# Queries and keys by seven half products, sums on GpSimd, divisions on ScalarE, and output groups spread over the steps

## The chip, the cores and the metric

The kernel runs on one core of a Trainium2 chip. The core has a matrix engine (TensorE, PE in the profile, with PEld for its weight loads), a vector engine (VectorE, DVE), a scalar engine (ScalarE, ACT), a general engine (GpSimd, POOL) and a queue engine that issues transfers (SyncE, SP). They run at the same time and wait for one another by semaphores. The metric is the device time of the whole program in microseconds. The three runs of the kernel before took 3513.65, 3513.8 and 3515.68 us, a median of 3513.8.

## The reference, cut to what matters

Two attention layers follow each other. Each normalises its input by groups, projects it to queries, keys and values, adds relative-position terms to the scores, and adds the projected output to its input. There are 4 images of 32 x 32 tokens with 768 channels, and 12 heads of 64 channels. All of it is float32.

```python
qkv = x @ Wqkv                                   # (4, 1024, 768) @ (768, 2304)
q, k, v = split by 3, heads of 64
rel_h = einsum('bhwc,hkc->bhwk', r_q, Rh)        # position terms from the queries
rel_w = einsum('bhwc,wkc->bhwk', r_q, Rw)
scores = scale * (q @ k.T) + rel_h[..., :, None] + rel_w[..., None, :]
out = softmax(scores) @ v
x = x + (out @ Wproj + bproj)
```

In the second layer the projections have a bias, and the scale is applied to q as well.

## The kernel before, in words

**Tiling.** An image of one layer is 6 chunks of 128 channels by 1024 tokens. The 8 image passes (2 layers of 4 images) are numbered `im`. The heads go in pairs: 6 pairs per pass, 48 in all, numbered `g`. A pair's scores are cut into 8 units of 128 query rows, numbered `n`; a unit holds both heads. So there are 384 steps, each of one unit, in the loop over `units` (L562).

**What a step holds.** The engines' order is written by hand (`manual_schedule`, L539): each engine does its instructions in the order of the Python calls. In a step for unit `n` of pair `g` come: the small things left over from two steps before (`early`), the position terms of the unit two ahead (`biases`, GpSimd, L323), the scores of the unit one ahead (`scores`: L337 on TensorE, L346 on VectorE which adds the position terms and takes the row's extreme, L350 on ScalarE for the exponential), the reads of turned probabilities that are due (`behind`), the transposition of unit `n` (`turn`: L370 on VectorE, its write to memory L372 on SP), the division of the unit one ahead (`divide`: L358, one head on GpSimd at L362 and one on ScalarE at L364), and then a share of other matrix work out of a list `todo` (`take`). In step 6 and in step 2 of the next pair `weigh` multiplies the probabilities with the values (L399, `av`). What it reads from memory, `pt`, is fetched a quarter (two units) at a time by `read_back` (L381): units 0 and 1 in step 3, 2 and 3 in step 4, 4 and 5 in step 7, 6 and 7 in step 0 of the next pair.

**The list of other matrix work.** `prepare(g + 1)` gives the projections of the next pair: `project_in` makes queries and keys, each in two halves of 512 tokens (L215); `project_values` makes the values of two pairs in four groups, two of them per pair (L250). `put_out` gives groups of the output projection (L471), four per pair, 12 steps of `take` together. `shares` (L567) says how many pieces are taken in each step: 6, 6, 0, 6, 12, 6, 0, 12. So in a usual pair the queries are made in steps 0 and 1, the keys in 3 and 4, values in 4 and 5, and all the output groups in step 7.

**Half-height matmuls.** L215 and L250 split each chunk of 128 channels into two halves of 64 rows. The two halves go to different row halves of the matrix engine and to two accumulators, and a ScalarE copy (L228 or L230) and a VectorE sum (L231) bring them together. The scores (L337) and the position products (L282, `tp`) also use half the rows, for one head each. The output projection uses all 128 rows.

**Buffers.** `ps_m` has two accumulators for all groups but the scores, so a group's accumulator is wanted again two groups later. `ps_s` has two for the scores of the two heads. The position products go through memory: `positions` copies a part of them, ScalarE writes it (L289), and `diagonals` reads it back shifted, in eight reads of SP (L309) for the whole pair, into `rel`, which `biases` reads.

**Between images.** The statistics of the next image are collected during pairs 0 to 2, its group statistics are exchanged in pair 3 (`norm`), and its chunks are normalised by VectorE in pair 4 (`apply`, L194).

Of the kernel before, what the change touches and what calls it, by code (L numbers as in the profile page):

```python
# [50 lines left out]
AHEAD = 3  # L51
# [3 lines left out]
def attention_blocks(ctx: ExitStack, tc: tile.TileContext, a: dict, out: bass.AP):  # L55
# [4 lines left out]
    wpool = ctx.enter_context(tc.tile_pool(name="weights", bufs=2))  # L60
    wopool = ctx.enter_context(tc.tile_pool(name="wo", bufs=2))
    xpool = ctx.enter_context(tc.tile_pool(name="x", bufs=NC + AHEAD))
    apool = ctx.enter_context(tc.tile_pool(name="attn", bufs=6))
    qkpool = ctx.enter_context(tc.tile_pool(name="qk", bufs=2))
    vpool = ctx.enter_context(tc.tile_pool(name="v", bufs=3))
    scpool = ctx.enter_context(tc.tile_pool(name="sc", bufs=6))
    tmppool = ctx.enter_context(tc.tile_pool(name="tmp", bufs=2))
    tbpool = ctx.enter_context(tc.tile_pool(name="tb", bufs=2))
    ptpool = ctx.enter_context(tc.tile_pool(name="pt", bufs=2))
    relpool = ctx.enter_context(tc.tile_pool(name="rel", bufs=2))  # L70
    iopool = ctx.enter_context(tc.tile_pool(name="io", bufs=4))
# [15 lines left out]
    xn_of, w_of, wo_of = {im: [] for im in range(NI)}, {}, {}  # L87

    def load_x(im, c, chunk=None):

        l, b = images[im]
        if c == len(xn_of[im]):
            xn_of[im].append(xpool.tile([P, S], FP, tag="xn", name=f"xn_{im}_{c}"))
        chunk = c if chunk is None else chunk
        nc.sync.dma_start(out=xn_of[im][c], in_=srcs[l][b][chunk * P : (chunk + 1) * P, :])

    def load_w(g, which):

        im, pair = divmod(g, NP)
        if which == 2:  # L100
            w = wpool.tile([P, NC, 2 * P], FP, tag="wv", bufs=1, name=f"wv_{g}")
            src = a[f"wv{images[im][0]}"][pair // 2]
        else:
            w = wpool.tile([P, NC, P], FP, tag="w", name=f"w_{g}_{which}")
            src = a[f"wqk{images[im][0]}"][pair, which]
        w_of[g, which] = w
        nc.sync.dma_start(out=w, in_=src.rearrange("p (c o) -> p c o", c=NC))

    for c in range(NC):
        load_x(0, c)  # L110
    for which in range(3):
        load_w(0, which)
# [35 lines left out]
    def stats(im, c, i, x):  # L148

        if i == 0:  # L150
            half_stats[im] = small.tile([P, 2, 6], FP, tag="st", name=f"st_{im}_{c}")
        st = half_stats[im]
        nc.vector.bn_stats(st[:, i, :], x)  # L153
        if i == 1:
            nc.vector.bn_aggr(mv_of[im][:, c, :], st.rearrange("p i s -> p (i s)"))

    def norm(im):
# [26 lines left out]
        def inverses():  # L184
            nc.vector.reciprocal(mv[:, 2, 0:1], mv[:, 2, 1:2])
            for k, x in enumerate((mv[:, 0, 0:1], mv[:, 2, 0:1])):
                nc.vector.tensor_copy(g[:, 1, :, k], x.to_broadcast([NG, GS]))
# [5 lines left out]
        def apply(c):  # L193
            nc.vector.tensor_scalar(  # L194
                xn_of[im][c], xn_of[im][c], nrm[:, c, 0:1], nrm[:, c, 1:2], ALU.subtract, ALU.mult
            )

        return {1: gather, 2: by_group, 4: groups, 5: inverses, 7: spread}, apply

# [3 lines left out]
    def project_in(g, which, i):  # L203

        im, pair = divmod(g, NP)
        xn, w = xn_of[im], w_of[g, which]
        cols = slice(i * HALF, (i + 1) * HALF)
        if i == 0:
            tag = "qk"[which]
            qk_of[g, which] = qkpool.tile([P, S], FP, tag=tag, name=f"{tag}_{g}")  # L210
        t = ps_m.tile([P, 2, HALF], FP, tag="m", name=f"pj_{g}_{which}_{i}")
        for c in range(NC):
            for a in range(2):
                rows = slice(a * D, (a + 1) * D)
                nc.tensor.matmul(  # L215
                    t[:, a, :], lhsT=w[rows, c, :], rhs=xn[c][rows, cols],
                    start=(c == 0), stop=(c == NC - 1),
                )
            if c < NC - 1:
                yield True  # L220
# [49 lines left out]
    def positions(g, i):  # L270
# [27 lines left out]
        if i == 1:  # L298
            later.append(lambda: diagonals(g))
# [386 lines left out]
```

## Time and profile before

| | |
|---|---|
| median of three runs | 3513.8 us |
| the profiled execution, its own time | 3513.09 us |
| span from the first to the last instruction | 3511.3 us |
| granted TensorE clock | 0.998 |
| PE busy | 3460.9 us, 99% of the span |
| DVE busy | 2306.5 us, 66% |
| POOL busy | 2290.3 us, 65% |
| ACT busy | 1810.3 us, 52% |
| transfers, share of 16 engines (largest queue) | 82.9% |

A line of the groups view gives the line of the code, the engine, the operation, what it writes and reads, the shape and the count; then the busy time and the mean of one in ns; then the idle time just before, with what ended it. A line of the chain of work that ended last gives shares of the span. A line of a timeline gives the start, the length and what ran. Each matmul of the code is two instructions in the profile. Matmul ends are modelled, so distances between starts say more than busy time.

### The profile page before, as it was taken

How to read it: one execution, taken by the hardware profiler on the slowest of the kernel's cores; microseconds unless marked ns; L12 is line 12 of the kernel's file. 1: busy time of each engine (PE TensorE's matmuls, PEld its weight loads, DVE VectorE, ACT ScalarE, POOL GpSimd, SP SyncE). 2: the span in 40 equal slices, each digit the busy share in tenths (PEclk: the TensorE clock that was granted, in tenths of full speed). 3: DMA queues.
4: the chain of work that ended last, by engine and by line, in shares of the span. 5: the costliest groups of instructions: out<-in, count | busy, mean ns of one | idle time of the engine just before them, and what ended most of it. 6: DMA issues, size and time to landing. Idle time of an engine off the chain costs nothing.

```text
span 3511.3 us, 55069 instructions
## 1 busy us (share of the span) xinstructions
PE 3460.9 (99%) x21120; PEld 1920.0 (55%) x21120; DVE 2306.5 (66%) x3532; ACT 1810.3 (52%) x2913; POOL 2290.3 (65%) x1154
## 2 busy tenths in 40 slices
PE   6999999999999999999999999999999999999998
PEld 3555555555555555555555555555555555555553
DVE  4766767767677676666766667666666666666665
ACT  3555545554545545455545555455545555455543
POOL 3776666666666666666666666666666666666662
PEclk9999999999999999999999999999999999999999
DMA  3988988889898888988888988888888888888877
GB/s 129 321 299 290 322 306 308 316 285 316 301 321 308 295 313 290 320 303 285 310 306 314 305 287 309 311 305 300 297 305 316 307 292 301 310 297 291 293 275 264
DMA packets 520407, 1046.75 MB, mean 298 GB/s; under 512 B 142672, under 2 KB 205648, under 8 KB 470992
## 3 DMA queue, kind: packets, MB, share of 16 engines
q1 hardware_dynamic: 465648, 1015.81, 82.9%
q10 hardware_dynamic: 54496, 27.43, 2.6%
q8 instruction: 166, 2.72, 0.3%
q14 instruction: 97, 0.79, 0.1%
HBM read 568.01 MB, written 475.10 MB: 297 GB/s over the span
## 4 chain that ended last, share of the span: by engine, by line
PE 94%; DVE 2%; DMA 2%; issue 1%; ACT 0%; SPq 0%; DVEq 0%; ACTq 0%
PE pj L215 26%; PE av L399 19%; PE s L337 19%; PE pv L250 14%; PE o L471 14%; PE tp L282 2%; DMA td<-tb 1%; DVE tb L370 1%; DVE sc L346 1%; DMA pt<-td 0%; DVE st L153 0%; DVE q L231 0%; DVE res L482 0%; DMA per<-mv 0%; ACT q L230 0%
## 5 line engine op out<-in xcount | busy, mean ns | idle before, releaser
L323 POOL TENSOR_TENSOR sc<-rel 128x1024 f32<-128x1024 f32 x768 | 1881.2, 2473 | 48.3 <-DMA rel<-tdr 33.6
L350 ACT ACTIVATE sc<-sc,sm 128x1024 f32<-128x1024 f32 x768 | 880.3, 1147 | 792.1 <-DVE sm L346 790.6
L346 DVE CUSTOM_DVE_ANT_0 sc<-s,sc 128x1024 f32<-128x1024 f32 x768 | 908.2, 1220 | 438.3 <-issue 221.5
L362 POOL TENSOR_SCALAR sc<-sc,sm 128x1024 f32<-128x1024 f32 x376 | 420.3, 1118 | 1099.5 <-DVE sm L358 1069.0
L215 PE MATMUL pj<-xn,w 64*128 64x512 f32 x4608 | 1032.5, 591 | 26.9 <-DVE xn L194 25.9
L370 DVE STREAM_TRANSPOSE tb<-sc 128x1024 f32<-128x1024 f32 x768 | 907.9, 1220 | 14.6 <-DMA td<-tb 12.9
L215 PEld LDWEIGHTS pj<-xn,w 64*128 64x128 f32 x4608 | 452.2, 188 | 569.3 <-issue 527.6
L337 PE MATMUL s<-k,q 64*128 64x512 f32 x3072 | 751.1, 598 | 6.6 <-DVE sm L346 6.4
L364 ACT ACTIVATE sc<-sc,sm 128x1024 f32<-128x1024 f32 x392 | 449.2, 1148 | 499.6 <-DVE sm L358 499.6
L399 PE MATMUL av<-pt,v 128*64 128x256 f32 x6144 | 684.7, 381 | 10.1 <-DVE q L231 7.7
L399 PEld LDWEIGHTS av<-pt,v 128*64 128x64 f32 x6144 | 432.9, 137 | 291.6 <-DVE q L231 41.6
L250 PE MATMUL pv<-wv,xn 64*128 64x256 f32 x4608 | 515.7, 376 | 0.0
L250 PEld LDWEIGHTS pv<-wv,xn 64*128 64x128 f32 x4608 | 448.7, 187 | 90.5 <-issue 33.4
L471 PE MATMUL o<-attn,wo 128*128 128x512 f32 x1080 | 476.3, 597 | 0.0
L337 PEld LDWEIGHTS s<-k,q 64*128 64x128 f32 x3072 | 288.7, 187 | 299.9 <-issue 268.8
L471 PEld LDWEIGHTS o<-attn,wo 128*128 128x128 f32 x1080 | 201.5, 190 | 271.4 <-issue 254.9
L261 DVE TENSOR_TENSOR v<-pv,v 128x256 f32<-128x256 f32 x192 | 81.5, 425 | 240.1 <-ACT v L260 240.1
L231 DVE TENSOR_TENSOR k<-pj,k 128x512 f32<-128x512 f32 x96 | 66.4, 692 | 182.3 <-ACT k L228 93.1
L231 DVE TENSOR_TENSOR q<-pj,q 128x512 f32<-128x512 f32 x96 | 66.4, 692 | 171.8 <-ACT q L230 85.9
L260 ACT COPY v<-pv 128x256 f32<-128x256 f32 x192 | 70.5, 367 | 189.8 <-PE pv L250 142.7
L297 ACT COPY rel<-tp 32x256 f32<-32x256 f32 x384 | 139.4, 363 | 53.9 <-ACT t L287 27.8
L350 ACT ACTIVATION_READ_ACCUMULATOR sc<-sc,sm 128x1 f32 x768 | 143.2, 187 | 0.0
(36 smaller groups left out, 941.7 us busy)
## 6 DMA issues: line engine op xcount, KB each, us to landing
td<-tb SPq DMA_DIRECT2D x384, 1024.0 KB, 5.7
pt<-td SPq DMA_DIRECT2D x382, 1024.0 KB, 8.8
w<-in_wqk SPq DMA_DIRECT2D x96, 384.0 KB, 5.7
tdr<-t ACTq DMA_DIRECT2D x96, 256.0 KB, 8.0
part<-res SPq DMA_DIRECT2D x84, 256.0 KB, 4.7
res<-part SPq DMA_DIRECT2D x84, 256.0 KB, 7.5
wv<-in_wv SPq DMA_DIRECT2D x24, 768.0 KB, 6.6
wo<-in_wo SPq DMA_DIRECT2D x90, 192.0 KB, 7.1
```

What stands on the lines that cost most here:

```text
L215: nc.tensor.matmul(t[:, a, :], lhsT=w[rows, c, :], rhs=xn[c][rows, cols], start=(c == 0), stop=(c == NC - 1),)
L250: nc.tensor.matmul(t[:, a, k, :], lhsT=xn[c][rows, (2 * i + k) * P : (2 * i + k + 1) * P], rhs=w[rows, c, :], start=(c == 0), stop=(c == N ...
L297: nc.scalar.copy(rel_of[g][rows, :, 0, 4 * i : 4 * i + 4, :], src)
L323: nc.gpsimd.tensor_tensor(sc.rearrange("p (a k) (u l) -> p a (k u) l", a=4, l=8), rel[:, h, 0, n, :].unsqueeze(1).unsqueeze(3).to_broadcas ...
L337: nc.tensor.matmul(ps[h][:, cols], lhsT=q[rows, n * P : (n + 1) * P], rhs=k[rows, cols], start=True, stop=True,)
L346: nc.vector.tensor_tensor_reduce(out=sc, in0=ps[h], in1=sc, scale=-scale, scalar=BIG, op0=ALU.add, op1=ALU.min, accum_out=st[:, 0, h : h + 1],
L350: nc.scalar.activation(sc, sc, AF.Exp, bias=st[:, 0, h : h + 1], scale=-1.0, accum_out=st[:, 1, h : h + 1],)
L362: nc.gpsimd.tensor_scalar(sc, sc, st[:, 2, h : h + 1], 1.0, ALU.mult, ALU.mult)
L364: nc.scalar.mul(sc, sc, st[:, 2, h : h + 1])
L370: nc.vector.transpose(tb[:, :, h, :], sc_of[g, n, h])
L399: nc.tensor.matmul(av[rows, at * 2 * P : (at + 1) * 2 * P], lhsT=v_of[g][:, k, rows], rhs=pt_of[g, quarter].rearrange("p n r k h i -> p (n ...
L471: nc.tensor.matmul(t, lhsT=wo_of[im, o, c], rhs=attn_of[im * NP + c][:, cols], start=(c == c0), stop=(c == c1 - 1),)
```

## The change: what it does

Queries and keys together are one product of the normalised image with a weight matrix of 256 columns. It is now cut in two along all three sides: the tokens in halves x0 and x1, the channels in chunks 0 to 2 and 3 to 5, and the columns in queries (`wa`) and keys (`wc`). That would be eight products of half matrices. The changed kernel computes them as seven, from sums and differences of the halves (the scheme of Strassen and Winograd). Each of the seven is three matmuls over whole chunks of 128 rows.

GpSimd makes the sums of operands: of the weights once per pair (`combine`), of the image once per image (`sums`, spread over the steps in `sum_steps`), and of the value weights once per two pairs (`combine_values`), since the second half of the image is kept as a sum afterwards. VectorE adds up the products (seven sums per pair in place of four, L293 and L295 of the changed kernel), and ScalarE keeps one copy of a product in place of four. The bias of the second layer is added in VectorE's sums.

The divisions of both heads go to ScalarE, except for the first head of units 2 and 4, which stays on GpSimd. Normalisation goes to ScalarE (`scale` and `bias` of an activation) in pair 4, and is spread over the steps in `applies`. The image is held and loaded in halves of tokens. The diagonals are read in two halves of eight reads each, the first in step 3 and the second in step 0 of the pair itself. The list of other matrix work is mixed by `merge`: product 0 and one output group, values, values, product 1, one output group, products 2 and 3, two output groups, with shares 9, 6, 0, 6, 9, 9, 0, 6. In the opening, all groups of pair 0 are done ahead of the loop.

```diff
-    wpool = ctx.enter_context(tc.tile_pool(name="weights", bufs=2))
+    wpool = ctx.enter_context(tc.tile_pool(name="weights", bufs=1))
-    xpool = ctx.enter_context(tc.tile_pool(name="x", bufs=NC + AHEAD))
+    xpool = ctx.enter_context(tc.tile_pool(name="x", bufs=3 * NC))
-    vpool = ctx.enter_context(tc.tile_pool(name="v", bufs=3))
+    vpool = ctx.enter_context(tc.tile_pool(name="v", bufs=4))
-    tmppool = ctx.enter_context(tc.tile_pool(name="tmp", bufs=2))
+    tmppool = ctx.enter_context(tc.tile_pool(name="tmp", bufs=1))
+    spool = ctx.enter_context(tc.tile_pool(name="sums", bufs=NC // 2))
...
+    def combine(g, stage):
+
+        wa, wc, t1, t2, t4 = (weights_of(g, name) for name in "ac124")
+        sub = lambda to, x, y: nc.gpsimd.tensor_tensor(to, x, y, ALU.subtract)
+        if stage == 0:
+            sub(t1, wc[:, :NB], wa[:, :NB])
+            sub(wc[:, :NB], wc[:, NB:], wc[:, :NB])
+        else:
+            sub(t2, wc[:, NB:], t1)
+            sub(t4, wa[:, NB:], t2)
+
+    def combine_values(g):
+
+        w = wv_of[g]
+        nc.gpsimd.tensor_tensor(w[:, NB:], w[:, NB:], w[:, :NB], ALU.subtract)
...
-        def apply(c):
-            nc.vector.tensor_scalar(
-                xn_of[im][c], xn_of[im][c], nrm[:, c, 0:1], nrm[:, c, 1:2], ALU.subtract, ALU.mult
+        def apply(c, h, scalar=True):
+            x = xn_of[im][h][c]
+            if scalar:
+                nc.scalar.activation(x, x, AF.Identity, bias=nrm[:, c, 1:2], scale=nrm[:, c, 0:1])
+            else:
+                nc.vector.tensor_scalar(
+                    x, x, nrm[:, c, 0:1], nrm[:, c, 1:2], ALU.mult, ALU.add
+                )
...
+    def sums(im, which, c):
...
+        to, x, y = {
+            1: lambda: (x1[c], x1[c], x1[c + NB]),
+            2: lambda: (s(2), x1[c], x0[c]),
+            3: lambda: (s(3), x0[c], x1[c]),
+            4: lambda: (s(4), x0[c + NB], s(2)),
+        }[which]()
+        nc.gpsimd.tensor_tensor(to, x, y, ALU.add if which == 1 else ALU.subtract)
...
-    def project_in(g, which, i):
+    def products(g, kind):
...
+        ops = {
+            0: ((wa, x0), (wa[:, NB:], x0[NB:])),
+            1: ((t2, s2), (wc, s3)),
+            2: ((t1, x1), (t4, x1[NB:])),
+            3: ((wc[:, NB:], s4),),
+        }[kind]
+        for h, (w, x) in enumerate(ops):
+            for c in range(NB):
                 nc.tensor.matmul(
-                    t[:, a, :], lhsT=w[rows, c, :], rhs=xn[c][rows, cols],
-                    start=(c == 0), stop=(c == NC - 1),
+                    t[:, h, :], lhsT=w[:, c, :], rhs=x[c], start=(c == 0), stop=(c == NB - 1),
                 )
...
+        ts = [turned(x) for x in ts]
+        if kind == 0:
+            nc.scalar.copy(kept, ts[0])
+            add(turned(qs[0]), ts[1], kept, 0)
+            (later if g else mid).append(lambda: positions(g, 0))
+        elif kind == 1:
+            add(ks[0], ts[0], kept)
+            add(ks[1], ts[1], ks[0])
+        elif kind == 2:
+            add(turned(qs[1]), ts[1], ks[1], 0)
+            add(ks[0], ts[0], ks[0])
+            add(ks[1], ts[0], ks[1], 1)
+            (later if g else mid).append(lambda: positions(g, 1))
+        else:
+            add(ks[0], ts[0], ks[0], 1)
...
-        if i == 1:
-            later.append(lambda: diagonals(g))
+        later.append(lambda: diagonals(g, i))
...
-            if h == 0 and not last:
+            if h == 0 and n in (2, 4) and not last:
                 nc.gpsimd.tensor_scalar(sc, sc, st[:, 2, h : h + 1], 1.0, ALU.mult, ALU.mult)
             else:
                 nc.scalar.mul(sc, sc, st[:, 2, h : h + 1])
...
+        values = [(project_values(first, i + k), NC) for k in range(2)]
+        groups = [(products(g, kind), NC if kind < 3 else NB) for kind in range(4)]
+        return groups[:1] + values + groups[1:]
+
+    def merge(ins, outs):
+
+        if not ins or not outs:
+            return ins + outs
+        return ins[:1] + outs[:1] + ins[1:4] + outs[1:2] + ins[4:] + outs[2:]
...
+    applies = {
+        2: ((0, 0), (0, 1), (0, 2)), 3: ((0, 3),), 4: ((0, 4), (0, 5), (1, 0)),
+        5: ((1, 3), (1, 1), (1, 4)), 7: ((1, 2), (1, 5)),
+    }
+    sum_steps = {
+        (4, 5): ((3, 0),),
+        (4, 6): ((1, 0), (2, 0), (3, 1)),
+        (4, 7): ((1, 1), (2, 1)),
+        (5, 0): ((3, 2), (1, 2), (2, 2)),
+        (5, 1): ((4, 0),),
+        (5, 2): ((4, 1), (4, 2)),
+    }
...
-                shares = [6, 6, 0, 6, 12, 6, 0, 12]
+                shares = [9, 6, 0, 6, 9, 9, 0, 6] if g >= 3 else [6, 6, 0, 6, 6, 9, 0, 0]
...
+            if n in (0, 2) and g + 1 < NPAIR:
+                combine(g + 1, n // 2)
+            if n == 4 and pair % 2 and g + 1 < NPAIR:
+                combine_values(g + 1)
+            if pair == 4 and not end:
+                for h, c in applies.get(n, ()):
+                    apply(c, h)
+            if not end:
+                for which, c in sum_steps.get((pair, n), ()):
+                    sums(im + 1, which, c)
             take(todo, share)
```

## The prediction

> **What bounds the kernel now.** I read the page first: part 1 for the busy shares, part 4 for what carries the end.
>
> ```profile
> PE 3460.9 (99%) x21120; PEld 1920.0 (55%) x21120; DVE 2306.5 (66%) x3532; ACT 1810.3 (52%) x2913; POOL 2290.3 (65%) x1154
> ...
> PE 94%; DVE 2%; DMA 2%; issue 1%; ACT 0%; SPq 0%; DVEq 0%; ACTq 0%
> PE pj L215 26%; PE av L399 19%; PE s L337 19%; PE pv L250 14%; PE o L471 14%; PE tp L282 2%; DMA td<-tb 1%; DVE tb L370 1%; DVE sc L346 1%; DMA pt<-td 0%; DVE st L153 0%; DVE q L231 0%; DVE res L482 0%; DMA per<-mv 0%; ACT q L230 0%
> ```
>
> TensorE is the bound, everything else has a third of its time free, and the lines edited (`pj`) are 26% of the chain. Busy matmul ends are modelled, so I priced from starts: the timeline of TensorE, over one pair of heads in the middle (start, us, group).
>
> ```profile
> 1528.76 1.88 PE L337 MATMUL s<-k,q 64*128 64x512 f32 x8
> 1530.58 7.13 PE L399 MATMUL av<-pt,v 128*64 128x256 f32 x64
> 1537.63 1.99 PE L337 MATMUL s<-k,q 64*128 64x512 f32 x8
> 1539.55 10.57 PE L471 MATMUL o<-attn,wo 128*128 128x512 f32 x24
> 1550.05 1.99 PE L337 MATMUL s<-k,q 64*128 64x512 f32 x8
> 1551.87 5.32 PE L215 MATMUL pj<-xn,w 64*128 64x512 f32 x24
> 1557.02 1.88 PE L337 MATMUL s<-k,q 64*128 64x512 f32 x8
> 1558.74 5.32 PE L215 MATMUL pj<-xn,w 64*128 64x512 f32 x24
> 1563.89 1.06 PE L282 MATMUL tp<-tab,q 64*128 64x128 f32 x16
> 1564.78 1.89 PE L337 MATMUL s<-k,q 64*128 64x512 f32 x8
> 1566.59 7.13 PE L399 MATMUL av<-pt,v 128*64 128x256 f32 x64
> 1573.65 1.16 PE L282 MATMUL tp<-tab,q 64*128 64x128 f32 x16
> ```
>
> Groups follow without a hole. A pair takes 71.7 us (scores at 1502.95 and again at 1574.65). A matmul in the code is two instructions here (4608 `pj` for 48 x 48). The `pj` group of 24 half-height instructions takes 5.15 us, 0.429 per two; the 24 full-height ones of `o` take 10.50.
>
> The groups view prices the other engines.
>
> ```profile
> L323 POOL TENSOR_TENSOR sc<-rel 128x1024 f32<-128x1024 f32 x768 | 1881.2, 2473 | 48.3 <-DMA rel<-tdr 33.6 <-DVE tb L370 14.7
> L362 POOL TENSOR_SCALAR sc<-sc,sm 128x1024 f32<-128x1024 f32 x376 | 420.3, 1118 | 1099.5 <-DVE sm L358 1069.0 <-DMA td<-tb 30.5
> L364 ACT ACTIVATE sc<-sc,sm 128x1024 f32<-128x1024 f32 x392 | 449.2, 1148 | 499.6 <-DVE sm L358 499.6
> L194 DVE TENSOR_SCALAR xn<-xn,nrm 128x1024 f32<-128x1024 f32 x48 | 84.0, 1770 | 3.5 <-DMA nrm<-back 3.5
> L231 DVE TENSOR_TENSOR q<-pj,q 128x512 f32<-128x512 f32 x96 | 66.4, 692 | 171.8 <-ACT q L230 85.9 <-ACT q L228 85.8
> ```
>
> Last, the timelines of VectorE and of SP for two dates that the new order leans on: the last eviction of a value group, and the eight reads of the position diagonals.
>
> ```profile
> 1530.92 0.42 DVE L261 TENSOR_TENSOR v<-pv,v 128x256 f32<-128x256 f32 x1 [0.44 <-ACT v L260]
> ```
> ```profile
> 1513.15 4.13 SPq L309 DMA_DIRECT2D rel<-tdr  x8
> ```
>
> **What the skill says.** The Trainium skill, TensorEngine Tiling (Array Packing), Key Properties: row tiles run in parallel, but changing the tiling mode drains the engine. The trace agrees and prices it: weight loads inside the `o` block stand 0.429 us apart, so 24 cost 10.30; two score blocks among row-tiled work cost 1.72 each (1557.02 to 1558.74); but scores, `o`, scores take 14.24 (1537.63 to 1551.87). The excess is 0.50, and 0.11 of it is the way out of `av` (`tp` takes 1.00 after `av`, 0.89 otherwise). **A full-height block costs 0.39 us to enter and leave.** SBUF — State Buffer, Who interferes with whom: a VectorE tensor_scalar in a two-port mode and a GpSimd operation lock each other out; L194 takes 806 ns at least and 1770 in the mean, which agrees.
>
> **The change, part by part.** S is the start of a step's scores.
>
> *1. Seven products.* Per pair 48 matmuls over half chunks become 21 over whole ones. 4608 x 0.2146 = 989 us become 2016 x 0.429 = 865: -123.5. Half-height work ran two at a time, so nothing is lost by it before; all the gain is the eighth product (20.6 to 18.0 us per pair).
>
> *2. Mode switches.* Full-height blocks per pair: now one (`o`). After, in the emitted order: product 0 with an output group (step 0), product 1 with an output group (4), products 2 and 3 (5), two output groups (7): four. Over the run, 44 pairs with outputs gain three, three early ones gain three, the opening two: 143 x 0.39 = +56.
>
> *3. Image boundaries.* The DVE normalisations delay the eviction of q before `av` in the pair after; the gap from the last score to `av` is 1.58 to 1.77 us seven times against 0.52 usually. They go to ScalarE and are spread: -8.
>
> *4. VectorE.* Four sums per pair of 692 ns become seven: +2.1 us per pair on an engine that is busy 47.6 of 71.7. They end before the PSUM buffer is wanted: the three after product 2 end at S+9.1 of step 5 and `av` takes that buffer at S+11.3. Nothing. If this cover went, each 0.69 us late would be 33 us.
>
> *5. ScalarE.* 282 divisions come (1.148 each, +324), three of four evictions per pair go (-92 at 0.57 to 0.68), 84 normalisations come (priced like L230, 0.67: +56): 2100, 62%. What matters is the queue: an eviction behind two divisions starts 1.15 us later. The sharpest place is step 1, a value group, whose buffer `av` wants in step 2 with only `tp` and scores between. But unit 2's first half is divided on GpSimd still, so ScalarE stands as in the old step 5: scores 1521.87, last sum over at 1531.34, S+9.47. `av` can start at S+9.57 (1557.02 to 1566.59). Slack 0.1 us: nothing, or +0.1 to 0.3 us per pair.
>
> *6. GpSimd.* 282 divisions go (-315). Sums of 384, 512 and 768 elements come, 192, 96 and 24 of them. The trace has none of these shapes; below, L323 scaled by size gives 0.93, 1.24, 1.85 us; above, a line through L323 and the 4497 ns for 2048 elements of the Trainium skill (GPSIMD Engine Reference, Performance versus the Vector engine) gives estimates of 1.21, 1.46, 1.97. I take the upper: +419, total 2394, 68 to 70%. They stand behind biases that are due two steps later. The fullest spell (step 6 of one pair to step 2 of the next at a boundary) sums to 46 us in 43 us of steps against a lead of one step, 9 us. Nothing. If it were late, VectorE's L346 waits, then TensorE at the next scores.
>
> *7. Queues.* The diagonals are read in two halves, so SP issues eight more per pair, and the x loads double in number at the same bytes. The second eight now stand in step 0 ahead of the reads of pt for units 6 and 7. With the table's write issued 2.1 us after its `tp` starts and landing 8.8 later, eight issues of at most 4.1, two stores: pt is issued some 16 us after `tp`, lands 9 to 10 later (paired reads: 9.9 in the median), at 26; `av` wants it at 27.2 (step 7's 8.0 after `tp`, step 0 9.7, step 1 6.9, and 2.7). Now the slack in this place is 3.6 in the median. About 1.5 us remain: nothing, at worst some stalls.
>
> *8. Opening and end.* Values move into the opening (+5.2, taken out of step 0), and `tp` waits for the first eviction (1.3) where it waited for nothing; the cheaper products and one group's restart balance it: 0, bounded by -3 and +3. The end is the same work.
>
> Sum: -123.5 + 56 - 8 = -75.5, and +3 for the thin margins of 5 and 7. The profiled execution took 3513.1 us with a span of 3511.3, and the median is 3513.8: 3513.1 - 72.5 = 3440.6, so 3440 as a time.
>
> **Rivals.** *Switches cost less* (only the hole at the switch itself, 0.1 us each way, the rest hidden): 143 x 0.2 = 29 instead of 56, 3413. For it: the bare start-to-start gap at a switch is only 0.52 against 0.43. Against: the 14.24 above. *The pt reads come late* (part 7): with another 2.5 us on them (lanes shared with 16 small reads, DMA at 0.90 share in this pair), step 2 of each pair waits 1 us: +48, 3488. For it: the reads of rel and the slack worked out; against: the smaller reads issue faster than the large ones. *It ends slower*: the same wait, 3.0 us long per pair, costs more than the gain; pt would have to land 4.5 us later than worked out, as where the table's write lands behind two pt reads and a td write instead of before them. At 3.0 us it is 3440 + 3.0 x 47 = 3581; it decides from 1.6 us of wait per pair (75.5 / 47). Against: the table's write landed within 10 us each time. *The change does nothing*: excluded, since TensorE is given 2592 fewer product instructions and is the engine without holes.
>
> **How the numbers follow.** Forecast case 0.62 (3425 to 3460 by the bounds of 5 to 8), cheap switches 0.13, pt late by about 1 us 0.14, slower 0.08, a wash of waits and gain 0.03. Leaving out the slower cases and the outer half of the late reads gives 3410 to 3482. A difference of 0.2% (7 us) is about what these runs can tell: faster 0.89, same 0.03, slower 0.08.
>
> **What will show it.** A middle pair at 70.3 us instead of 71.7; product blocks of 12 instructions in 5.2 us; scores 1.8 to 1.9 beside each; boundary pairs without their 1.1 us; TensorE still 94% of the chain. POOL sums of 384 elements at 0.93 to 1.21 us. Wrong if `av` L475 shows waits on pt or on v of over 0.3 us per pair, if the score sums wait for biases long enough to hold TensorE's scores, or if a full-height block costs other than 0.39.

## The result and the profile after

| | before | after |
|---|---|---|
| median | 3514.03 us (3513.65 to 3515.68) | 3460.43 us (3456.97 to 3462.95) |
| profiled execution, its span | 3511.3 us | 3459.5 us |
| granted TensorE clock | 0.998 | 0.995 |

The ratio is 0.9846, with a 95% interval of 0.9829 to 0.9863. The change is worth 53.6 us, where 73.8 were forecast. The time is inside the range that was given (3410 to 3482), 20 us above the point, and at the upper edge of what the forecast case alone allowed (3425 to 3460).

First, the page of the kernel after: the busy times, then the chain of work that ended last, by engine and by line.

```profile
PE 3401.9 (98%) x18528; PEld 1841.0 (53%) x18528; DVE 2366.2 (68%) x3642; ACT 2082.5 (60%) x3141; POOL 2327.1 (67%) x1184
...
PE 96%; DMA 1%; DVE 1%; issue 1%; ACT 0%; POOL 0%; SPq 0%; ACTq 0%; DVEq 0%; POOLq 0%
PE pj L280 25%; PE s L413 20%; PE av L475 19%; PE pv L330 14%; PE o L547 14%; PE tp L359 3%; DMA td<-tb 1%; DVE tb L446 0%; DVE sc L422 0%; DVE st L186 0%; DMA pt<-td 0%; DMA w_last<-in_wo 0%; ACT sc L440 0%; DMA per<-mv 0%; POOL sc L399 0%
```

The 2592 instructions fewer on PE are there, ScalarE took 272 us more, and TensorE is still the bound: 96% of the chain. Its busy time fell by 59 us and the span by 52, so some idle time has come in. Next, the timeline of TensorE over a middle pair, from one step's scores to the same step a pair later.

```profile
1532.38 1.99 PE L413 MATMUL s<-k,q 64*128 64x512 f32 x8
1534.29 5.42 PE L280 MATMUL pj<-xn,wa 128*128 128x512 f32 x12
1539.55 2.74 PE L547 MATMUL o<-attn,wo 128*128 128x512 f32 x6
1542.22 1.99 PE L413 MATMUL s<-k,q 64*128 64x512 f32 x8
...
1550.11 1.89 PE L413 MATMUL s<-k,q 64*128 64x512 f32 x8
1551.92 7.13 PE L475 MATMUL av<-pt,v 128*64 128x256 f32 x64
...
1575.72 1.99 PE L413 MATMUL s<-k,q 64*128 64x512 f32 x8
1577.64 5.42 PE L280 MATMUL pj<-xn,w 128*128 128x512 f32 x12
1582.89 2.74 PE L280 MATMUL pj<-s,wc 128*128 128x512 f32 x6
1585.56 1.99 PE L413 MATMUL s<-k,q 64*128 64x512 f32 x8
```

Scores, 18 full-height instructions, scores take 9.84 us (1575.72 to 1585.56): 1.72 for the scores, 7.72 for 18 times 0.429, and 0.40 to enter and leave. `av` follows its scores without a hole (1550.11 to 1551.92). First score sums of the pairs stand 70.3 us apart in 33 of the 41 pairs of images 1 to 7 that have a pair after them; that is the forecast pair.

The groups view of the kernel after prices what was new to the trace.

```profile
L440 ACT ACTIVATE sc<-sc,sm 128x1024 f32<-128x1024 f32 x674 | 742.8, 1143 | 440.1 <-DVE sm L434 440.1
L231 ACT ACTIVATE xn<-xn,nrm 128x512 f32<-128x512 f32 x90 | 66.9, 800 | 4.0 <-DMA nrm<-back 4.0
L255 POOL TENSOR_TENSOR s<-xn,xn 128x512 f32<-128x512 f32 x48 | 61.2, 1284 | 13.8 <-DVE xn L233 7.9 <-ACT xn L231 2.5 <-DMA td<-tb 1.8
L127 POOL TENSOR_TENSOR w<-wc,w 128x384 f32<-128x384 f32 x48 | 48.8, 1016 | 0.0
L138 POOL TENSOR_TENSOR wv<-wv 128x768 f32<-128x768 f32 x24 | 43.9, 1831 | 5.0 <-PE pv L330 5.0
L293 DVE TENSOR_TENSOR k<-pj,k 128x512 f32<-128x512 f32 x144 | 98.5, 700 | 9.0 <-PE pj L280 7.3
L293 DVE TENSOR_TENSOR q<-pj,k 128x512 f32<-128x512 f32 x24 | 27.5, 1144 | 13.4 <-PE pj L280 13.2
L293 DVE TENSOR_TENSOR q<-pj,q 128x512 f32<-128x512 f32 x24 | 26.3, 1096 | 73.7 <-ACT q L301 73.7
```

GpSimd's sums of 384 and 512 elements lie between the two bounds of the prediction, nearer the lower one (1.01 us in 0.93 to 1.21, 1.28 in 1.24 to 1.46). Those of 768 elements take 1.83 us, at the lower bound of 1.85. The sums of the queries take 1.1 us, those of the keys 0.70: same shape, same engine.

Where the 20 us went shows when the span is cut at the first score sums of the images and pairs. The forecast column divides the forecast's own terms: 1.4 us a pair, 1.1 us for each boundary (it falls into the last pair of images 0 to 6), and for the opening the eighth product less two switches. It also counts work that the new order moves from one stretch to another: the values' 5.2 us go from pair 0 to the opening, and 12 instructions of output groups (5.15 us) from the last stretch to pair 3 of image 0, because two of the four groups of a pair now stand before step 7. The 3 us for thin margins are in no row.

| stretch | before | after | difference | forecast |
|---|---|---|---|---|
| up to the first score sum | 58.7 | 64.1 | +5.4 | +3.4 |
| image 0, pair 0 | 63.8 | 63.6 | -0.2 | -6.6 |
| image 0, pairs 1 and 2 | 129.4 | 131.6 | +2.2 | -2.8 |
| image 0, pair 3 | 65.8 | 67.6 | +1.8 | +3.7 |
| image 0, pairs 4 and 5 | 144.5 | 140.6 | -3.9 | -3.9 |
| images 1 to 6 | 2588.2 | 2537.7 | -50.5 | -57.4 |
| image 7, pairs 0 to 4 | 358.5 | 351.6 | -6.9 | -7.0 |
| last pair and the end | 102.5 | 102.8 | +0.3 | -5.2 |

Four places lost something: the opening together with pair 0 (8.4 us), the next two pairs of image 0, which have no output groups (5.0), eight pairs in images 1 to 4 (6.5), and the last pair (5.5). These are 25 us; less the 1.9 that pair 3 of image 0 gained beyond its row, and the margin of 3, about 20 remain. Image 0 with its six pairs takes 403.4 us in both kernels. The waits view of TensorE tells the same (waited for, us in total, times, longest), first of before, then of after.

```profile
PE av L399 <- DVE q L231: 7.7, 7, 1.2
PE s L337 <- DVE sm L346: 6.4, 6, 1.4
```
```profile
PE s L413 <- DVE sm L422: 10.8, 6, 4.8
PE av L475 <- DMA pt<-td: 6.2, 1, 6.2
PE av L475 <- PE s L413: 4.4, 8, 0.6
```

The boundary waits (7.7 us) are gone as forecast. The waits for score sums, all six of them in the opening, image 0 and the last pair, grew from 6.4 to 10.8 us. One wait for pt of 6.2 us stands in the last pair, where before had two, of 1.3 us at most. The eight waits of 0.5 to 0.6 us are those of images 1 to 4; the view names TensorE's own scores there, but by the order of ends `av` waits for the values' sums (in one of them the last sum ends at 634.61 and `av` starts at 634.72).

### The profile page after: what moved, and what is told of

Its sections match the earlier page's. It is cut to its first block, busy times and chain, and to the rows that moved or that the text cites. A ratio compares the mean times of both kernels' runs of the same rounds, so it can differ in the third digit from the quotient of the medians.

```text
span 3459.5 us, 51561 instructions
## 1 busy us (share of the span) xinstructions
PE 3401.9 (98%) x18528; PEld 1841.0 (53%) x18528; DVE 2366.2 (68%) x3642; ACT 2082.5 (60%) x3141; POOL 2327.1 (67%) x1184
## 4 chain that ended last, share of the span: by engine, by line
PE 96%; DMA 1%; DVE 1%; issue 1%; ACT 0%; POOL 0%; SPq 0%; ACTq 0%; DVEq 0%; POOLq 0%
PE pj L280 25%; PE s L413 20%; PE av L475 19%; PE pv L330 14%; PE o L547 14%; PE tp L359 3%; DMA td<-tb 1%; DVE tb L446 0%; DVE sc L422 0%; DVE st L186 0%; DMA pt<-td 0%; DMA w_last<-in_wo 0%; ACT sc L440 0%; DMA per<-mv 0%; POOL sc L399 0%
## 5 line engine op out<-in xcount | busy, mean ns | idle before, releaser
L399 POOL TENSOR_TENSOR sc<-rel 128x1024 f32<-128x1024 f32 x768 | 1877.1, 2468 | 657.7 <-DVE tb L446 623.0
L426 ACT ACTIVATE sc<-sc,sm 128x1024 f32<-128x1024 f32 x768 | 879.7, 1147 | 693.5 <-DVE sm L422 692.2
L440 ACT ACTIVATE sc<-sc,sm 128x1024 f32<-128x1024 f32 x674 | 742.8, 1143 | 440.1 <-DVE sm L434 440.1
L413 PE MATMUL s<-k,q 64*128 64x512 f32 x3072 | 761.6, 608 | 10.9 <-DVE sm L422 10.8
L547 PE MATMUL o<-attn,wo 128*128 128x512 f32 x1080 | 490.7, 597 | 0.0
L413 PEld LDWEIGHTS s<-k,q 64*128 64x128 f32 x3072 | 273.6, 187 | 365.8 <-issue 260.3
L438 POOL TENSOR_SCALAR sc<-sc,sm 128x1024 f32<-128x1024 f32 x94 | 105.1, 1118 | 379.1 <-DVE sm L434 357.3
L280 PE MATMUL pj<-xn,wa 128*128 128x512 f32 x576 | 266.6, 613 | 26.6 <-DVE xn L233 26.6
L280 PE MATMUL pj<-s,wc 128*128 128x512 f32 x576 | 262.8, 592 | 0.0
L280 PE MATMUL pj<-xn,w 128*128 128x512 f32 x576 | 259.9, 601 | 0.0
L280 PEld LDWEIGHTS pj<-xn,wa 128*128 128x128 f32 x576 | 108.0, 194 | 182.5 <-issue 120.5
L280 PEld LDWEIGHTS pj<-xn,w 128*128 128x128 f32 x576 | 105.6, 190 | 150.9 <-issue 149.7
L280 PEld LDWEIGHTS pj<-s,wc 128*128 128x128 f32 x576 | 109.4, 190 | 137.8 <-issue 135.8
```

What stands on the lines that cost most here:

```text
L280: nc.tensor.matmul(t[:, h, :], lhsT=w[:, c, :], rhs=x[c], start=(c == 0), stop=(c == NB - 1),)
L399: nc.gpsimd.tensor_tensor(sc.rearrange("p (a k) (u l) -> p a (k u) l", a=4, l=8), rel[:, h, 0, n, :].unsqueeze(1).unsqueeze(3).to_broadcas ...
L413: nc.tensor.matmul(ps[h][:, cols], lhsT=q[rows, n * P : (n + 1) * P], rhs=k[rows, cols], start=True, stop=True,)
L426: nc.scalar.activation(sc, sc, AF.Exp, bias=st[:, 0, h : h + 1], scale=-1.0, accum_out=st[:, 1, h : h + 1],)
L438: nc.gpsimd.tensor_scalar(sc, sc, st[:, 2, h : h + 1], 1.0, ALU.mult, ALU.mult)
L440: nc.scalar.mul(sc, sc, st[:, 2, h : h + 1])
```

## The experiments

The theory after the result: the gain is the eighth product less the switches, as forecast, and the missing 20 us are local stalls. Each ratio below is to runs of before taken beside it, so small differences are read from the ratios; after's own are 0.9846 and, run once more, 0.9854. Rivals: the switches cost something else and another term hides it; or the extra divisions on ScalarE cost time all along.

**Whole chunks alone.** The kernel before, with its eight products made full-height and nothing else: four more blocks a pair, no other gain.

```diff
-            for a in range(2):
-                rows = slice(a * D, (a + 1) * D)
-                nc.tensor.matmul(
-                    t[:, a, :], lhsT=w[rows, c, :], rhs=xn[c][rows, cols],
+            nc.tensor.matmul(
+                t[:, 0, :], lhsT=w[:, c, :], rhs=xn[c][:, cols],
...
-        nc.vector.tensor_tensor(to, t[1], to, ALU.add)
```

> The kernel before with its eight query and key products over whole chunks: same array time (48 half-height pairs of 0.429 us become 48 full-height instructions of 0.429), no second accumulator to add, but each group now stands as a full-height block between half-height scores: four more blocks per pair and three in the opening, 191 in all. If a block costs 0.39 us to enter and leave: +74 us, about 3588. If only the hole at the switch counts (0.2 us per block): +38, about 3552. If switching costs nothing or whole chunks are the gain by themselves: 3514 or less.

Measured: 3578.16 us (3573.28 to 3585.20), ratio to before 1.0187 (1.0172 to 1.0202). The timeline of TensorE in this kernel:

```profile
1585.78 1.99 PE L334 MATMUL s<-k,q 64*128 64x512 f32 x8
1587.70 5.42 PE L213 MATMUL pj<-xn,w 128*128 128x512 f32 x12
1593.04 1.99 PE L334 MATMUL s<-k,q 64*128 64x512 f32 x8
```

Scores, product, scores take 7.26 us. The scores are 1.72 and the product 5.15 (12 times 0.429), so entering and leaving costs 0.39. Pairs take 73.3 us in place of 71.7, 1.6 for four blocks. The whole grew by 65 us, 9 less than expected from 191 blocks; at the seven boundaries pairs grow by 0.3 to 0.7 us and not by 1.6, since their wait of 1.1 us is gone here too. The price per block holds, and with it the term of +56 us; the rival of cheap switches falls.

**Divisions back on GpSimd.** The kernel after, with the first head of every unit divided on GpSimd as before.

```diff
-            if h == 0 and n in (2, 4) and not last:
+            if h == 0 and not last:
```

> The changed kernel with the division of the first head of every unit back on GpSimd. If TensorE's own work sets the time and GpSimd has room (2327 us busy of 3460, 2640 with the divisions back), the time stays at 3460 within 5 us. If the divisions had to go because GpSimd's sums would come late, above all in pairs 4 and 5 of an image, scores wait there: 7 boundaries by 3 to 10 us, 3480 to 3530.

Measured: 3459.11 us (3456.18 to 3460.66), ratio 0.9845 (0.9831 to 0.9860). Pairs stay at 70.3. The eight slow pairs of images 1 to 4 shrink to two, with 0.3 and 0.4 us over (1688.2 us from image 1 to image 5 against 1693.9), but image 1 begins at 472.1 us and not at 467.5: image 0 gives most of the gain back (its pair 0 takes 67.0 us in place of 63.6, its pair 3 takes 70.9 in place of 67.6, and pair 2 is 2.3 shorter). Moving the divisions to ScalarE is not what the gain rests on.

**All output groups in step 7.** The kernel after, with the output groups in one block again. The number of full-height blocks per pair stays at four.

```diff
-        return ins[:1] + outs[:1] + ins[1:4] + outs[1:2] + ins[4:] + outs[2:]
+        return ins + outs
-                shares = [9, 6, 0, 6, 9, 9, 0, 6] if g >= 3 else [6, 6, 0, 6, 6, 9, 0, 0]
+                shares = [6, 6, 0, 6, 6, 9, 0, 12] if g >= 3 else [6, 6, 0, 6, 6, 9, 0, 0]
```

> The changed kernel with all four output groups in step 7 again. There are still four full-height blocks per pair (product 0, product 1, products 2 and 3, outputs), so if blocks and array time decide: 3460 within 5 us, pairs of 70.3 us. If the even steps are what brings the gain (the longest step grows from 9.7 to 13 us), pairs grow by 0.5 us or more: 3485 and over.

Measured: 3507.03 us (3505.97 to 3511.43), ratio 0.9986 (0.9978 to 0.9995). Nearly the whole gain is gone: pairs take 71.5 us, so the second branch came, 47 us above the first. The waits view of this kernel, and then its timeline from the start of step 0:

```profile
PE av L475 <- issue: 55.6, 45, 2.1
```
```profile
1559.82 2.19 ACT L440 ACTIVATE sc<-sc,sm 128x1024 f32<-128x1024 f32 x2 [1.09 <-DVE sm L434]
...
1562.04 0.59 ACT L301 COPY q<-pj 128x512 f32<-128x512 f32 x1
1562.04 5.35 PE L330 MATMUL pv<-wv,xn 64*128 64x256 f32 x48
...
1562.65 1.10 DVE L293 TENSOR_TENSOR q<-pj,q 128x512 f32<-128x512 f32 x1 [2.87 <-ACT q L301]
1563.59 1.21 DVE L422 CUSTOM_DVE_ANT_0 sc<-s,sc 128x1024 f32<-128x1024 f32 x1
...
1570.63 0.42 DVE L342 TENSOR_TENSOR v<-pv,v 128x256 f32<-128x256 f32 x1 [0.44 <-ACT v L341]
...
1571.15 7.13 PE L475 MATMUL av<-pt,v 128*64 128x256 f32 x64 [1.16 <-issue]
```

`av` waits 45 times, 1.24 us in the mean. What it waits for is worked out from the order of ends: the last sum of the values ends at 1571.05, 0.1 us before it starts ("issue" is only the profile's word for a wait that it can't name). Back from there: step 0 is now product 0 alone, 7.3 us (1552.95 to 1560.22). Both divisions occupy ScalarE until 1562.01, the copy of the queries waits behind them, the queries' sum on VectorE behind the copy, and the score sum behind that. It starts 3.4 us after the scores of its step, where after has 2.1, and everything behind it is as late. In after the output group behind product 0 makes step 0 9.8 us long, and the same chain is hidden under it.

**The same with GpSimd's division.** If ScalarE's queue is the cause, one division less in step 0 must help.

```diff
-            if h == 0 and n in (2, 4) and not last:
+            if h == 0 and not last:
```

> All output groups in step 7 as in the 3507 us run, but the first head's division on GpSimd in every step, as before the change. Theory (the output group behind product 0 is only cover for ScalarE, which does both divisions of step 0 for 2.19 us ahead of the queries' eviction and so sends everything behind it 1.4 us late): with one division less on ScalarE in step 0 the eviction comes 1.1 us earlier, the wait of TensorE before the values' sums in step 2 falls from 1.8 us to 0.5 to 0.9 a pair, and the time is 3460 to 3475 us. Rival (the spread itself is what counts: with product 0 alone in step 0 TensorE reaches step 2 too early for the reads of the transposed scores, whoever divides): pairs stay at 71.5 and the time at 3500 to 3508.

Measured: 3474.22 us (3472.80 to 3475.68), ratio 0.9890 (0.9876 to 0.9905): 33 us of the 47 come back, and pairs fall from 71.6 to 70.5, except pair 3 of images 1 to 6, which rises to 72.0 to 72.2. The theory holds for the larger part; the wait is ScalarE's two divisions ahead of the eviction. So "most divisions on ScalarE" and "output groups spread over steps" belong together: the first costs the better part of the gain unless the second covers it.

Pair 3 is where the next image's group statistics are exchanged, and VectorE shows something else there, first in this kernel, then in after:

```profile
733.41 3.96 DVE L222 COPY g<-gmv 32x24 f32<-32x24 f32 x2
```
```profile
733.56 0.28 DVE L222 COPY g<-gmv 32x24 f32<-32x24 f32 x2
```

Two copies of 32 x 24 elements take 1.55 and 2.49 us in place of 0.16 and 0.17, and each ends with one of two position terms of GpSimd (L399, which end at 734.93 and 737.35). In after GpSimd stands idle there, from 731.56 to 735.07. So it is in all seven exchanges of this kernel. The transposes and the sums of products 2 and 3 stand behind the copies, and the next `av` starts 1.43 us late. That it is late because of them is read from the order of ends; no run moves the copies alone.

**Queries summed in their own order.** After keeps tokens of the keys and of the first product in an order with four-way strides. Here the queries are written contiguously, and the operands that don't fit are read with strides.

```diff
-            nc.scalar.copy(kept, ts[0])
-            add(turned(qs[0]), ts[1], kept, 0)
+            nc.scalar.copy(qs[1], ts[0])
+            add(qs[0], ts[1], qs[1], 0)
...
-            add(ks[0], ts[0], kept)
+            add(ks[0], turned(ts[0]), turned(qs[1]))
...
-            add(turned(qs[1]), ts[1], ks[1], 0)
+            add(rowed(qs[1]), rowed(ts[1]), natural(ks[1]), 0)
```

> The changed kernel with the sums that make the queries written in order (the kept product stored in order and read with a stride instead). In the changed kernel these sums, written with a stride of four, take 1.10 to 1.23 us, against 0.70 of the others. If the strided write is the cost: 0.70 to 0.77 us here, the wait of the opening's tp for q shrinks by 0.4, the waits of 0.6 us behind product 0 in pairs 0 and 1 of images 1 and 2 go: 3455 to 3459. If a strided read costs the same, or the shape of the instruction does: 1.1 us stays, 3460.

Measured: 3457.41 us (3455.74 to 3458.96), ratio 0.9843 (0.9827 to 0.9859), against 3460.43 for after: too little to be told from it. The stalls shrink and don't go: pairs 1 and 2 of images 1 to 4 fall by about 0.3 us each, 2.7 us from image 1 to image 5. The groups view of this kernel:

```profile
L294 DVE TENSOR_TENSOR k<-pj,k 128x512 f32<-128x512 f32 x144 | 96.8, 687 | 8.4 <-PE pj L280 6.7
L294 DVE TENSOR_TENSOR k<-pj,q 128x512 f32<-128x512 f32 x48 | 53.4, 1113 | 5.4 <-PE pj L280 3.7
L294 DVE TENSOR_TENSOR q<-pj,k 128x512 f32<-128x512 f32 x24 | 26.0, 1083 | 11.9 <-PE pj L280 11.6
L294 DVE TENSOR_TENSOR q<-pj,q 128x512 f32<-128x512 f32 x24 | 16.6, 691 | 73.9 <-ACT q L301 73.9
```

The first sum of the queries fell from 1096 to 691 ns, and a sum of the keys rose from 679 to 1113, because it now reads the kept product with a stride from SBUF. The second sum of the queries stays at 1083, because here it reads the keys with a stride (of 1 KB). A strided operand in SBUF, read or written, costs 0.4 us at 512 columns. The first row reads PSUM with the same stride and pays nothing.

**The opening's queue.** In after, ScalarE issues the second half of pair 0's diagonals for one head, just ahead of the first exponential.

```diff
-                (nc.scalar if h and not g else nc.sync).dma_start(
+                (nc.scalar if h and not g and not i else nc.sync).dma_start(
```

> After, with the second half of pair 0's diagonals all read on SyncE's queue and none on ScalarE's. Theory (four DMA issues, 1.8 us, and a table load behind them hold up the first exponential and all that follows in the opening): first exponential at 66.5 to 67 us in place of 68.52, the 5.4 us gap between the scores at 83 us falls to about 2 us, and the time falls by 2 to 5 us, to 3455 to 3458. Rival (the opening is bounded by VectorE and GpSimd, and the queue is covered): first score sums of image 1 still at 467 us, time 3460.

Its timeline and, below, that of after:

```profile
65.74 1.28 ACT L426 ACT_TABLE_LOAD   x1
67.03 1.15 ACT L426 ACTIVATE sc<-sc,sm 128x1024 f32<-128x1024 f32 x1
...
87.34 3.83 PE L413 MATMUL s<-k,q 64*128 64x512 f32 x7 [2.86 <-DVE sm L422]
```
```profile
65.38 1.81 ACTq L385 DMA_DIRECT2D rel<-tdr  x4
...
67.22 1.28 ACT L426 ACT_TABLE_LOAD   x1 [2.42 <-issue]
68.52 1.15 ACT L426 ACTIVATE sc<-sc,sm 128x1024 f32<-128x1024 f32 x1
...
88.83 4.07 PE L413 MATMUL s<-k,q 64*128 64x512 f32 x7 [4.85 <-DVE sm L422]
```

The first exponential comes 1.5 us earlier although this opening began 1.1 us later; the wait of the scores falls from 4.85 to 2.86, and pair 0 takes 60.6 us in place of 63.6. Yet the median is 3459.99 us (3455.97 to 3463.38), ratio 0.9850 (0.9834 to 0.9867). Only 1.6 us reach image 1 in the profiled execution: of the 3.0 us of pair 0, the later opening takes 0.9 and pair 2 of image 0 takes 0.5. There `av` waits, at 210 us, where it starts 2.65 us after the last score instruction and not 0.52. The theory holds for pair 0; that the program gains from it isn't shown by this run.

**Reads of pt first.** SP issues the reads of the transposed scores in step 0 ahead of the diagonals.

```diff
+            if n == 0:
+                run(behind[0])
             run(early)
```

> After, with the reads of the transposed scores of a pair's last units issued on SyncE ahead of the diagonals, residuals and weights of step 0 and not behind them. Theory (in the last pair these reads stand behind a 6.8 us burst of diagonals and weights): the 6.4 us gap in the weighted sums at 3377 us falls to 1 to 2 us and the time by 4 to 5 us, to 3455.5 to 3456.5; the other pairs stay at 70.3. Rival (the gap comes from the late exponentials and writes of the last pair, not from the order on the queue, or the diagonals now come late and GpSimd's sums with them): the gap stays or moves to the next score product, time 3458 to 3463.

Measured: 3460.05 us (3458.16 to 3462.18), ratio 0.9850 (0.9836 to 0.9865). The hole in `av` at 3377 us falls from 6.6 to 3.5, and a second one of 3.4 us opens at 3405 us, because now the diagonals come late and GpSimd waits for them. GpSimd waits 8.5 us for them, in after 2.4. The expectation of 4 to 5 us missed; the queue's order moves the wait on.

**Statistics at the end of their step.** In pairs 0 to 2 of images 1 to 4, the statistics of new rows (L186) stand on VectorE ahead of the transposes. Here `stats` in `project_out` is held back until the end of the step.

```diff
-            stats(im + B, o, i, to)
+            after_step.append(lambda: stats(im + B, o, i, to))
...
             take(todo, share)
+            run(after_step)
```

> After, with the statistics of the new rows (48 instructions of 0.70 us on VectorE in images 0 to 3, ahead of the transposes of their step) moved to the end of their step. Theory (they make the reciprocal of step 7 late, and so both divisions, the queries' eviction and the values): pairs 1 and 2 of images 1 to 4 go from 70.9 and 71.7 us to 70.3, the time falls by 5 to 7 us to 3453.5 to 3455.5. Rival (the evictions of the output groups themselves make it late): pairs stay at 70.9 and 71.7, time 3460.

Measured: 3458.34 us (3457.65 to 3461.74), ratio 0.9847 (0.9832 to 0.9862). Pairs 1 and 2 of images 1 and 2 fall from 70.9 and 71.7 us to 70.6 and 71.4, those of images 3 and 4 from about 70.9 to 70.6 and 70.7: 2.0 us of 6.5. The statistics are a third of the cause. The order of the queries' sums was worth 2.7 us in its own run, and GpSimd's divisions in all steps 5.7. Which step's division it is, and what the evictions of the output groups cost, these runs don't separate.

**Together.** One kernel takes three edits (queries in order, opening's queue, statistics). Another takes these, divides the first head of unit 7 on GpSimd in pairs 0 to 2 of images 1 to 7, and asks for the last output weights (`fetch_last`) two steps earlier, in step 6 of pair 46. After ran once more beside them.

```diff
-            if h == 0 and n in (2, 4) and not last:
+            if h == 0 and (n in (2, 4) or n == 7 and g >= NP and g % NP < 3) and not last:
...
-                        fetch_last()
...
+            if n == 6 and g + 2 == NPAIR:
+                fetch_last()
```

> The kernel after once more, to stand beside the two kernels that gather the edits: 3457 to 3463 us.

> The first three of these edits (queries in their own order, the opening's diagonals, the statistics): the stalls of pairs 1 and 2 in images 1 to 4 gone or at 0.3 us a pair, the gap at 3377 us as in after. 3449 to 3454 us. If the division of step 7 is what makes the stalls, pairs 1 and 2 of images 1 and 2 stay at 70.6 and 71.4 and the time at 3455 or more.

> Five edits in one: queries summed in their own order, the opening's diagonals on SyncE alone, the statistics at the end of their step, the first head's division of step 7 on GpSimd in pairs 0 to 2 of images 1 to 7, and the last weights asked for two steps earlier, in step 6 of pair 46. Sums expected from the single runs: opening 2 to 4 us, stalls of images 1 to 4 6 to 7 us, gap at 3377 us 3 to 4 us (the burst of diagonals, 6.8 us beside the weights' transfers in the last pair, should be 3.7 us as in the middle pairs). Together 11 to 15 us: 3445 to 3450. If the edits only hand each other's waits on, 3455 or more.

| | median | ratio to before |
|---|---|---|
| after, once more | 3462.61 us (3461.95 to 3464.55) | 0.9854 (0.9841 to 0.9867) |
| three edits | 3454.83 us (3453.10 to 3455.41) | 0.9830 (0.9817 to 0.9844) |
| five edits | 3452.52 us (3450.20 to 3453.03) | 0.9823 (0.9810 to 0.9837) |

Five edits beat after by 10.1 us, with no overlap of the runs, a little less than the 11 to 15 expected. The stalls of images 1 to 4 shrink by 4.7 us with three edits, which is the sum of the two single runs (2.7 and 2.0). With five they shrink by the same 4.7: pair 2 of images 1 and 2 stays at 71.1 in both. The division was meant for step 7, but the edit names unit 7, which is divided in step 6. The trace of the five, for pair 0 of image 1, has one division of unit 7 on GpSimd (scores in step 6, at 524.69), and both of the next unit (scores in step 7, at 534.66) still on ScalarE:

```profile
531.62 1.12 POOL L438 TENSOR_SCALAR sc<-sc,sm 128x1024 f32<-128x1024 f32 x1 [6.05 <-DVE sm L434]
...
542.40 2.19 ACT L440 ACTIVATE sc<-sc,sm 128x1024 f32<-128x1024 f32 x2 [2.06 <-DVE sm L434]
```

So step 7's division was never moved alone. What five edits gain over three lies in the last pair (98.3 us against 102.2) and is the weights' part: SP's and TensorE's timeline, first of five edits, then of after.

```profile
3359.71 4.51 SPq L385 DMA_DIRECT2D rel<-tdr  x8
...
3373.97 5.26 PE L475 MATMUL av<-pt,v 128*64 128x256 f32 x32 [2.45 <-DMA pt<-td]
```
```profile
3367.35 6.83 SPq L385 DMA_DIRECT2D rel<-tdr  x8
...
3383.52 5.52 PE L475 MATMUL av<-pt,v 128*64 128x256 f32 x32 [6.24 <-DMA pt<-td]
```

Without the weights in front of it the burst of diagonals takes 4.5 us and not 6.8, and `av` waits 2.5 us and not 6.2. With three edits `av` still waits 6.0 us. Image 7 with the end is 449.9 us with five edits and 453.8 with three; the kernels that leave the end as in after took 451.1 to 454.8. The runs of five and of three do not overlap, with 2.3 us between the medians.

## Why the prediction was right, and where it lost 20 us

**Seven products, switches, boundaries (steps 1 to 3): right.** 70.3 us a pair is -2.6 for the eighth product and 3 times 0.39 for the switches, to a tenth. The run with whole chunks alone measured the switch by another route at 0.39. The boundary waits of 7.7 us are gone from the waits view.

**VectorE (step 4): right in the sum, wrong in the price.** Seven sums of 692 ns were assumed; the two sums of the queries take 1.10 to 1.23 us with their stride. In the middle pairs the cover holds.

**ScalarE (step 5): the weak place was another one.** I looked at step 1 and its slack of 0.1 us. The run with all output groups in step 7 shows the sharp one in step 0, where the copy of product 0 stands behind two divisions: uncovered, it costs most of 47 us, of which 33 come back with one division less. The forecast time didn't suffer, since the order as emitted puts an output group there, but I had not named that as the cover. In pairs 1 and 2 of images 1 to 4, where output groups and statistics crowd VectorE in step 7, the same chain stalls in after too: 6.5 us. The normalisation was priced at 0.67 us and takes 0.80.

**GpSimd and the reads of pt (steps 6 and 7): right.** Sums of 1.01, 1.28 and 1.83 us lie inside the bounds or at the lower one, and in no middle pair does TensorE wait for GpSimd or for pt. VectorE's score sums do wait for the image's sums, seven times and 29.8 us in all, without holding TensorE. The slack of pt in step 2, from the last landing to the start of `av`, is about 1.9 us in the median and 0.2 at least, forecast 1.5. For the kernel before, the prediction put it at 3.6; counted the same way it is 5.0, so this change used up more of it than was thought.

**Opening and end (step 8): this step failed.** "0, bounded by -3 and +3" was missed by 8 us in the opening and pair 0 together. Up to the first score sum it is +5.4, where the terms give +3.4: TensorE is 3.8 us longer busy there (35.48 against 31.70 us), and the rest is a restart 0.8 us later and the wait for the first eviction. I had taken the values' 5.2 us out of pair 0 again, but pair 0 took 63.6 us and not 57: it is not bounded by TensorE. What was taken out became the wait of 4.85 us. The run with the opening's queue shows that the four issues are part of it: 3.0 us of pair 0 went with them in its profile. The rest stays open.

Pairs 1 and 2 of image 0 were given the gain of the middle pairs too (the sum took 143 blocks and 48 products as if TensorE carried every pair), and that is another 5.0 us. They have no output groups, so step 0 holds product 0 alone, as in the run with the groups in step 7. The table by stretch (length; busy times of PE, PEld, DVE, ACT and POOL with counts; granted clock; DMA share; GB/s), of before, of after, and of the run with pt first, for pair 1 of image 0 each:

```profile
122.50:186.30 63.80, 62.38 (x416) 36.01 (x416) 44.53 (x70) 36.69 (x60) 47.40 (x25) 1.00 0.90 316
```
```profile
127.70:193.50 65.80, 64.35 (x362) 34.88 (x362) 46.83 (x74) 41.44 (x64) 46.82 (x23) 0.95 0.84 300
```
```profile
127.70:191.50 63.80, 61.07 (x362) 34.69 (x362) 46.83 (x73) 40.73 (x62) 46.35 (x23) 1.00 0.85 303
```

At full clock the pair takes 63.8 us in both kernels. TensorE is busy 1.3 us less in the new one and waits as much longer: `av` of step 2 starts 1.9 us after the last score instruction in place of 0.5. In after the pair takes 65.8. At the end of step 7 two score instructions start 2.0 us apart, and behind them matmuls stand 0.85 to 1.0 us apart in place of 0.43 for some 5 to 7 us; the pair's mean clock is 0.95. Its first product shows it, where 12 instructions took 5.42 us in the middle pair:

```profile
132.97 7.81 PE L280 MATMUL pj<-xn,wa 128*128 128x512 f32 x12
```

Before has the hole too, and its clock was 1.00 in two of its first three pairs and 0.97 in the third. What decides whether the clock drops after such a hole stays open. The run with all output groups in step 7 has the order of after in this pair, and took 63.8 us at a clock of 1.00.

"The end is the same work" was wrong as well. The last stretch had 5.15 us of output groups less to do and still took 0.3 us more: eight reads of diagonals now stand with the weights ahead of the last reads of pt on SP, and the longest wait of `av` for pt grew from 1.3 us to 6.2.

**Rivals.** Cheap switches: refuted by 0.39 measured twice. pt late in each pair: no such waits in the middle pairs. Slower by the same wait: also not seen. A wait of 1.2 us a pair in step 2 does exist, but on the values and not on pt, and only once the cover in step 0 is taken away. The measured time lies between the forecast and late reads (3488), but no reads of pt in the middle pairs made it so.

## What to carry to other kernels

Price a change of a tiled TensorE by the pair that repeats, but sum the opening, the pairs without filler work and the end apart: a gain of TensorE is only a gain where TensorE is the bound. Where an edit puts work on an in-order queue ahead of an eviction, follow the chain from that queue to the next matmul in every step, and name the filler that hides it, since an innocent reordering of the filler can cost what the edit gained. Small waits can hand each other on, as in image 0 and in the last pair, or add up, as the stalls of images 1 to 4 did (2.7 and 2.0 us alone, 4.7 together); only a trace of both edits tells which. Of five single edits of the kernel after, none moved the median by more than 3.0 us; three of them together with the earlier weights were worth 10. And look in the trace whether an edit moved the instruction that it was meant for.

## What the runs showed of the hardware that was not expected

- A VectorE sum of 512 columns with an SBUF operand at a 16-byte stride takes 1.10 to 1.14 us (written) or 1.11 (read), with one read at a 1 KB stride 1.08, against 0.68 to 0.70; the 16-byte stride on its PSUM operand costs nothing.
- A full-height block among row-tiled matmuls costs 0.39 to 0.40 us for entering and leaving together, for blocks of 12 and of 18 instructions alike; a block of 24 had given 0.39 in the kernel before.
- After two starts 2.0 us apart TensorE ran its next matmuls at half speed (0.85 us apart against 0.43) for some 5 to 7 us in pair 1 of image 0 in nine of the eleven profiles of after and its variants, at 65.8 us a pair; in two it did not, at 63.8.
- Two VectorE copies of 32 x 24 elements took 3.96 us together where two GpSimd sums ran beside them, each copy ending with one of the sums, and 0.28 us where GpSimd was idle.
- ScalarE's scale-and-bias activation from SBUF to SBUF takes 0.80 us for 512 columns, its copies out of PSUM 0.59 and its activations with a bias out of PSUM 0.67.
